# A low-rank weight mix: the plain weight enters the PSUM bank by a ScalarE copy in place of a VectorE addition

## The chip, the core and the metric

The kernel runs on one core of a Trainium2 chip. A core has five engines with queues of their own: TensorE (PE; its weight loads are listed as PEld), VectorE (DVE), ScalarE (ACT), GpSimd (POOL) and SyncE (SP), which here only issues transfers. TensorE writes its products into PSUM, a small memory of banks; a bank holds 128 partitions x 512 fp32 numbers. All other data on the core is in SBUF. The metric is the device time of one execution in microseconds (us), lower is better.

## The reference

```
x  : (2, 1024, 1024);  xn = layernorm(x)
s  = xn @ (weight * block_mask).T + bias                    # 32x32 blocks, about 0.3 of them on
coeffs[b] = softmax((mean_s(xn[b]) @ Wq.T) @ keys.T / sqrt(128))   # 8 experts
y  = xn @ W_org.T + sum_e coeffs[b, e] * (xn @ down[e]) @ up[e]    # rank 64 each
out = x + s * silu(y)
```

The sum over the experts is linear, so for each of the two batches (b = 0, 1) the kernel mixes one weight of 1024 x 1024, `W_org.T + down * (coeffs[b] * up)`, with `down` 1024 x 512 and `up` 512 x 1024, and then multiplies the activations by it. All of it is in fp32: the kernel splits each operand into a high part (rounded to the fp32r form that TensorE takes) and a low part (the rest), and makes three products per pair: high by high, high by low, low by high.

## The kernel before

**The mix.** A mixed weight is made in 16 pieces of 128 x 512: two halves of the columns (h = 0, 1), eight rows of tiles each (kt = 0 to 7). One piece goes through these functions:

- `y_prep` (line 373): SP loads the piece's `down` tile (`ds`) and the plain weight's piece (`wo`) into tiles of the pool `stage`, which has six tiles of one size, shared by all that is staged. ScalarE casts the high part (`dhi`, line 380), VectorE subtracts for the low part (`dlo`, line 381); each has two buffers.
- `y_mul` (line 384): 12 matmuls of 128 x 128 by 128 x 512 into one PSUM bank `psw` (two buffers): four groups of 128 ranks (the tiles `cut`, made by `scale_up`, lines 364 to 368, from the rows of `up` times the coefficients), three products each.
- `y_sum` (line 394): VectorE adds the bank to the plain weight's piece in SBUF (line 396).
- `y_hi` (line 398) and `y_lo` (line 405): for batch 0 the sum is split again, by a ScalarE cast (line 399) and a VectorE subtraction (line 407), into the weight slot that the later tiles multiply by. `y_add` is `y_sum` and `y_hi`, `y_fin` all three.

**The stages.** From the start to about 68 us the kernel loads, normalises and turns the activations and makes the masked product s of batch 0's first half of the columns. Then come:

1. The first mix (b, h) = (0, 0), lines 812 to 820: eight `y_mul` in a row, with each one's `y_sum`, the `y_prep` of the piece two on, `y_hi` and `y_lo` behind it.
2. The second mix (0, 1), `mix_jobs` and `jobs_b`: eight output tiles of 128 x 512 (24 matmuls each, `gemm`) that multiply by the first mixed weight, and after each of them one `y_mul`. A tile's evacuation and a piece's addition are put in a list `pending`, which `flush` issues ahead of the next tile.
3. Eight tiles that multiply by the second mixed weight, while VectorE, ScalarE and DMA prepare batch 1 (`wide_a`, `wide_b`: 1024-wide rows are normalised, added, and stored to a DRAM tensor `xv`) and the coefficients of batch 1.
4. The folds, `fold` (line 955): the 16 pieces of batch 1's mixed weight, in groups of 4, 4, 3, 3 and 2 with a tile of s (`s_tile`) ahead of each group. The sum is not split: it is stored from the `wo` tile to a DRAM tensor `yu` by a transfer that ScalarE issues one fold later (`store_late`). Between them stand `fill`s, which load prepared rows back and split them (lines 984 to 986). After the eighth fold `scale_up` makes the tiles `cut` for the other half of the columns, through four tiles of `stage`.
5. Batch 1's tiles (`quad`), from about 312 us to the end, which use a scheme with seven products in place of eight.

**What sets the order.** The whole body stands in a manual schedule: TensorE, VectorE, ScalarE and GpSimd run their instructions in the order in which the program issues them. Only SP's transfers, and which tile of a pool is handed out next, are placed by the framework. An engine that waits holds up all that stands behind it in its queue.

Of the kernel before, what the change touches and what calls it, by code (L numbers as in the profile page):

```python
# [9 lines left out]
F32 = mybir.dt.float32  # L10
# [4 lines left out]
ALU = mybir.AluOpType  # L15
AX = mybir.AxisListType

P = 128
# [4 lines left out]
NH = 512  # L23
# [9 lines left out]
def kernel(  # L33
# [26 lines left out]
    nc = tc.nc  # L60
# [23 lines left out]
    stage = for_fold("stage", 2)  # L84
    ps_acc = ctx.enter_context(tc.tile_pool(name="ps_acc", bufs=4, space=bass.MemoryType.PSUM))
    ps_w = ctx.enter_context(tc.tile_pool(name="ps_w", bufs=2, space=bass.MemoryType.PSUM))
# [101 lines left out]
    staged = {}  # L188
# [170 lines left out]
    def scale_up(b, h):  # L359
        cu[(b, h)] = []  # L360
        for c in range(4):
            t = cupool.tile([P, 2, NH], F32R, name="cut", tag="cu")
            st = stage.tile([P, NH], F32, name="us", tag="st", bufs=6)
            nc.sync.dma_start(st, up[c * P : (c + 1) * P, h * NH : (h + 1) * NH])
            s = csel[b][:, c : c + 1]
            hi = t[:, 0, :]
            nc.scalar.activation(hi, st, AF.Copy, scale=s)
            nc.vector.scalar_tensor_tensor(  # L368
                t[:, 1, :], st, s, hi.bitcast(F32), ALU.mult, ALU.subtract
            )  # L370
            cu[(b, h)].append(t)

    def y_prep(b, h, kt):
        ds = stage.tile([P, 4, P], F32, name="ds", tag="st", bufs=6)
        nc.sync.dma_start(ds, down[kt])
        ws = stage.tile([P, NH], F32, name="wo", tag="st", bufs=6)
        nc.sync.dma_start(ws, worgT[kt * P : (kt + 1) * P, h * NH : (h + 1) * NH])
        dhi = stage.tile([P, 4, P], F32R, name="dhi", bufs=2)
        dlo = stage.tile([P, 4, P], F32R, name="dlo", bufs=2)
        nc.scalar.copy(dhi, ds)  # L380
        nc.vector.tensor_tensor(dlo, ds, dhi.bitcast(F32), ALU.subtract)  # L381
        staged[(b, h, kt)] = dhi, dlo, ws

    def y_mul(b, h, kt):
        dhi, dlo, ws = staged[(b, h, kt)]
        u = cu[(b, h)]
        ps = ps_w.tile([P, NH], F32, name="psw", tag="psw")
        for c in range(4):
            nc.tensor.matmul(ps, lhsT=dhi[:, c, :], rhs=u[c][:, 0, :], start=c == 0, stop=False)  # L389
            nc.tensor.matmul(ps, lhsT=dhi[:, c, :], rhs=u[c][:, 1, :], start=False, stop=False)  # L390
            nc.tensor.matmul(ps, lhsT=dlo[:, c, :], rhs=u[c][:, 0, :], start=False, stop=c == 3)  # L391
        staged[(b, h, kt)] = ps, ws

    def y_sum(b, h, kt):
        ps, ws = staged[(b, h, kt)]
        nc.vector.tensor_tensor(ws, ws, ps, ALU.add)  # L396

    def y_hi(dst, b, h, kt):
        nc.scalar.copy(dst[:, kt, 0, :], staged[(b, h, kt)][1])

    def y_add(dst, b, h, kt):
        y_sum(b, h, kt)
        y_hi(dst, b, h, kt)

    def y_lo(dst, b, h, kt):
        ps, ws = staged.pop((b, h, kt))
        nc.vector.tensor_tensor(dst[:, kt, 1, :], ws, dst[:, kt, 0, :].bitcast(F32), ALU.subtract)

    def y_fin(dst, b, h, kt):
        y_add(dst, b, h, kt)  # L410
        y_lo(dst, b, h, kt)
# [44 lines left out]
    def tile_evac(kind, b, h, i, ps):  # L456
        mine = stash_p.tile([P, NH], F32, name="stash", tag="stash")
        if kind == "s":
            s_evac(mine, ps, b, i, h * NH, NH)
        else:  # L460
            y_evac(mine, ps, b, i)
        stash[(b, h, i)] = mine
# [14 lines left out]
    def store_late():  # L477

        while late_stores:
            nc.scalar.dma_start(*late_stores.pop(0))  # L480
# [3 lines left out]
    def flush():  # L484
        while pending:
            pending.pop(0)()
# [116 lines left out]
    with tc.manual_schedule(engines={mybir.EngineType.PE, mybir.EngineType.DVE, mybir.EngineType.Activation, mybir.EngineType.Pool}):  # L603
# [208 lines left out]
        for k in range(NKT):  # L812
            y_mul(0, 0, k)
            if k == 0:
                tile_evac("s", 0, 0, 7, q7)
            y_sum(0, 0, k)
            if k + 2 < NKT:
                y_prep(0, 0, k + 2)
            y_hi(y00, 0, 0, k)
            y_lo(y00, 0, 0, k)  # L820
# [132 lines left out]
        folds = [(h, kt) for h in range(2) for kt in range(NKT)]  # L953

        def fold(n):
            h, kt = folds[n]
            if n + 1 < len(folds):
                y_prep(1, *folds[n + 1])
            store_late()
            y_mul(1, h, kt)  # L960
            flush()
            y_sum(1, h, kt)
            ps, ws = staged.pop((1, h, kt))
            late_stores.append((
                yu[:, :, 2 * h + kt // 4, kt % 4, :].rearrange("u p n -> p u n"),
                ws.rearrange("p (u n) -> p u n", n=P),
            ))
            if n == NKT - 1:
                scale_up(1, 1)
# [297 lines left out]
```

## Time and profile before

| | us |
|---|---|
| median of 3 runs (461.96 to 462.08) | 461.96 |
| the profiled execution | 463.29 |
| its span, first to last instruction | 461.2 |
| TensorE busy | 443.0 |
| VectorE busy | 313.0 |
| ScalarE busy | 169.3 |

The span is a little shorter than the execution that it is from, since the time before the first and after the last instruction is not in it. Matmul rows overlap: each lasts about 0.39 us, and the next starts 0.227 us after it. In a line of the profile, `L396 DVE ... wo<-wo,psw ... x32 | 22.0, 686 | 17.3 <-PE psw L391 17.2` means: the instructions of line 396 on VectorE, which write `wo` and read `wo` and `psw`, 32 of them, busy for 22.0 us in all, 686 ns each; the engine was idle for 17.3 us just before them, of which 17.2 us ended when TensorE's line 391 had written `psw`. In a timeline the columns are start, length, engine, line, operation; the bracket at the end gives the idle time ahead of the instruction and what ended it.

### The profile page before, as it was taken

Reading aid. Unit: us, or ns where it says so; the run is one execution under the profiler, and the core shown is the slowest. Engines: PE = TensorE matmul, PEld = TensorE weight load, DVE = VectorE, ACT = ScalarE, POOL = GpSimd, SP = SyncE. Lnnn points to the kernel's source line nnn. Section 1 sums busy time; section 2 is a strip of 40 time slices with the busy share of each in tenths; the row PEclk is TensorE's granted clock in tenths of the full one; section 3 lists DMA queues with packets and bytes.
Section 4 is the critical chain, followed back from the end, with each engine's and each line's share of the span. In section 5 each row is a group of like instructions: output and inputs, shape, how many; then the busy total and the mean of one; then the engine's idle time right before and its main releaser. Section 6 shows DMA issues by size and latency. Waiting matters only on the chain.

```text
span 461.2 us, 5714 instructions
## 1 busy us (share of the span) xinstructions
PE 443.0 (96%) x2047; PEld 362.6 (79%) x2047; DVE 313.0 (68%) x504; ACT 169.3 (37%) x277; POOL 37.9 (8%) x40
## 2 busy tenths in 40 slices
PE   7799999999999999996999899999999999999996
PEld 5689888888887888874887688877888888888884
DVE  6989877667775788846555776769496196467624
ACT  4676534363223222214224223158343432441510
POOL 3884210000100000001000000000000000000000
PEclk9999999999999999998999999999999999999999
DMA  8996317687952688797887985664264134207003
GB/s 286 391 343 212 114 42 231 179 274 258 294 207 92 199 316 287 257 299 235 256 248 250 279 278 159 222 192 156 85 171 141 54 120 155 91 28 223 23 1 114
DMA packets 48172, 89.52 MB, mean 194 GB/s; under 512 B 4752, under 2 KB 14992, under 8 KB 48144
## 3 DMA queue, kind: packets, MB, share of 16 engines
q1 hardware_dynamic: 34512, 73.42, 49.1%
q10 hardware_dynamic: 13632, 15.73, 10.1%
q8 instruction: 16, 0.26, 0.2%
q14 instruction: 12, 0.10, 0.1%
HBM read 69.21 MB, written 19.92 MB: 193 GB/s over the span
## 4 chain that ended last, share of the span: by engine, by line
PE 74%; DVE 11%; DMA 10%; ACT 3%; issue 2%; SPq 0%; DVEq 0%; ACTq 0%
PE acc_ps L1127 22%; PE py L1127 9%; PE acc_ps L425 8%; PE acc_ps L427 8%; PE acc_ps L426 8%; PE psw L391 6%; PE psw L389 6%; PE psw L390 6%; DMA ws<-in_wT_dram 3%; DMA xv<-bd 2%; DMA xs<-xv 2%; DVE slot L544 1%; DMA raw<-in_x_dram 1%; DMA yu<-wo 1%; DMA us<-in_up_dram 1%
## 5 line engine op out<-in xcount | busy, mean ns | idle before, releaser
L1127 PE MATMUL acc_ps<-xw,ow 128*128 128x512 f32 x480 | 113.8, 393 | 0.7 <-ACT acc_ps L1158 0.4
L426 PE MATMUL acc_ps<-slot,xgrp 128*128 128x512 f32 (+1 forms) x288 | 105.8, 367 | 2.7 <-DVE slot L544 2.7
L1127 PEld LDWEIGHTS acc_ps<-xw,ow 128*128 128x128 f32 x480 | 90.0, 188 | 21.7 <-ACT acc_ps L1158 0.8
L425 PE MATMUL acc_ps<-slot,xgrp 128*128 128x512 f32 (+1 forms) x288 | 106.6, 370 | 0.1
L427 PE MATMUL acc_ps<-slot,xgrp 128*128 128x512 f32 (+1 forms) x288 | 105.6, 367 | 0.7 <-DVE xgrp L556 0.7
L426 PEld LDWEIGHTS acc_ps<-slot,xgrp 128*128 128x128 f32 x288 | 54.3, 189 | 12.2 <-DVE slot L544 3.6
L427 PEld LDWEIGHTS acc_ps<-slot,xgrp 128*128 128x128 f32 x288 | 54.2, 188 | 10.2 <-DVE xgrp L556 1.1
L425 PEld LDWEIGHTS acc_ps<-slot,xgrp 128*128 128x128 f32 x288 | 54.3, 188 | 9.1 <-DVE stash L439 0.3
L389 PE MATMUL psw<-cut,dhi 128*128 128x512 f32 x128 | 50.9, 398 | 4.5 <-ACT dhi L380 4.3
L391 PE MATMUL psw<-cut,dlo 128*128 128x512 f32 x128 | 50.9, 398 | 1.6 <-DVE dlo L381 1.5
L390 PE MATMUL psw<-cut,dhi 128*128 128x512 f32 x128 | 50.6, 395 | 0.0
L1127 PE MATMUL py<-xw,ow 128*128 128x512 f32 x192 | 46.9, 392 | 0.0
L1127 PEld LDWEIGHTS py<-xw,ow 128*128 128x128 f32 x192 | 36.1, 188 | 8.1
L1031 DVE TENSOR_TENSOR ow<-raw,ow 128x1024 fp32r<-128x1024 f32 (+1 forms) x32 | 34.5, 1089 | 11.2 <-ACT ow L1030 11.2
L380 ACT CAST dhi<-ds 128x512 fp32r<-128x512 f32 x32 | 19.8, 618 | 43.1 <-PE psw L390 24.3
L396 DVE TENSOR_TENSOR wo<-wo,psw 128x512 f32<-128x512 f32 x32 | 22.0, 686 | 17.3 <-PE psw L391 17.2
L389 PEld LDWEIGHTS psw<-cut,dhi 128*128 128x128 f32 x128 | 24.3, 190 | 10.2 <-ACT dhi L380 4.7
L391 PEld LDWEIGHTS psw<-cut,dlo 128*128 128x128 f32 x128 | 24.4, 191 | 8.4 <-DVE dlo L381 3.2
L1030 ACT CAST ow<-raw 128x1024 fp32r<-128x1024 f32 (+1 forms) x32 | 29.3, 939 | 2.0 <-DVE xw L986 2.0
L390 PEld LDWEIGHTS psw<-cut,dhi 128*128 128x128 f32 x128 | 24.3, 190 | 5.7 <-DVE cut L368 0.5
L381 DVE TENSOR_TENSOR dlo<-ds,dhi 128x512 fp32r<-128x512 f32 x32 | 21.9, 686 | 8.0 <-ACT dhi L380 8.0
L1172 DVE TENSOR_TENSOR py<-py,s 128x512 f32<-128x512 f32 x8 | 5.6, 699 | 29.6 <-ACT s L1134 29.4
(151 smaller groups left out, 451.6 us busy)
## 6 DMA issues: line engine op xcount, KB each, us to landing
ds<-in_down_dram SPq DMA_DIRECT2D x32, 256.0 KB, 3.7
wo<-in_worgT_dram SPq DMA_DIRECT2D x32, 256.0 KB, 3.9
raw<-in_x_dram SPq DMA_DIRECT2D x11, 512.0 KB, 6.3
res<-in_x_dram SPq DMA_DIRECT2D x16, 256.0 KB, 3.7
us<-in_up_dram SPq DMA_DIRECT2D x16, 256.0 KB, 3.6
out_dram<-res ACTq DMA_DIRECT2D x16, 256.0 KB, 3.6
raw<-in_wu_dram SPq DMA_DIRECT2D x8, 512.0 KB, 5.0
yu<-wo ACTq DMA_DIRECT2D x16, 256.0 KB, 4.0
```

Of the source, the lines that this page charges most:

```text
L380: nc.scalar.copy(dhi, ds)
L381: nc.vector.tensor_tensor(dlo, ds, dhi.bitcast(F32), ALU.subtract)
L389: nc.tensor.matmul(ps, lhsT=dhi[:, c, :], rhs=u[c][:, 0, :], start=c == 0, stop=False)
L390: nc.tensor.matmul(ps, lhsT=dhi[:, c, :], rhs=u[c][:, 1, :], start=False, stop=False)
L391: nc.tensor.matmul(ps, lhsT=dlo[:, c, :], rhs=u[c][:, 0, :], start=False, stop=c == 3)
L396: nc.vector.tensor_tensor(ws, ws, ps, ALU.add)
L425: nc.tensor.matmul(ps, lhsT=xs[:, kt, 0, cols], rhs=w[:, kt, 0, wc], start=kt == 0, stop=False)
L426: nc.tensor.matmul(ps, lhsT=xs[:, kt, 0, cols], rhs=w[:, kt, 1, wc], start=False, stop=False)
L427: nc.tensor.matmul(ps, lhsT=xs[:, kt, 1, cols], rhs=w[:, kt, 0, wc], start=False, stop=kt == NKT - 1)
L1030: nc.scalar.copy(o[:, a:b, 0], raw[:, a:b])
L1031: nc.vector.tensor_tensor(o[:, a:b, 1], raw[:, a:b], o[:, a:b, 0].bitcast(F32), ALU.subtract)
L1127: nc.tensor.matmul(ps, lhsT=o[:, a, wl, j, :], rhs=xw[j][:, m, xl, :], start=start and j == 0 and k == 0, stop=j == 3 and k == 2, skip_gro ...
```

## The change

The bank gets the plain weight first, by a ScalarE copy from SBUF (`y_seed`), and the matmuls then add to it: none of them starts the bank anew. The addition on VectorE goes. `y_hi` and `y_lo` read the sum from the bank itself. The first two pieces of the first mix stay as they were. Where no seed has been issued, `y_mul` issues it just ahead of its matmuls. In the folds the seed of the next piece is issued after this piece's matmuls, and as the sum is now in the bank, a ScalarE copy brings it to a new tile of `stage`, from which it is stored.

```diff
+    def y_seed(b, h, kt):
+        dhi, dlo, ws = staged[(b, h, kt)]
+        ps = ps_w.tile([P, NH], F32, name="psw", tag="psw")
+        nc.scalar.copy(ps, ws)
+        staged[(b, h, kt)] = dhi, dlo, ws, ps
+
     def y_mul(b, h, kt):
-        dhi, dlo, ws = staged[(b, h, kt)]
+        dhi, dlo = staged[(b, h, kt)][:2]
         u = cu[(b, h)]
-        ps = ps_w.tile([P, NH], F32, name="psw", tag="psw")
+        if (b, h) == (0, 0) and kt < 2:
+            ps = ps_w.tile([P, NH], F32, name="psw", tag="psw")
+        elif len(staged[(b, h, kt)]) == 3:
+            y_seed(b, h, kt)
+        seeded = len(staged[(b, h, kt)]) == 4
+        if seeded:
+            ps = staged[(b, h, kt)][3]
         for c in range(4):
...
+            for k, (d, ul) in enumerate(((dhi, 0), (dhi, 1), (dlo, 0))):
+                nc.tensor.matmul(
+                    ps, lhsT=d[:, c, :], rhs=u[c][:, ul, :], start=not seeded and c == 0 and k == 0, stop=c == 3 and k == 2,
+                    skip_group_check=seeded,
+                )
+        if not seeded:
+            ws = staged[(b, h, kt)][2]
+            nc.vector.tensor_tensor(ws, ws, ps, ALU.add)
+            ps = ws
+        staged[(b, h, kt)] = ps
 
-    def y_sum(b, h, kt):
-        ps, ws = staged[(b, h, kt)]
-        nc.vector.tensor_tensor(ws, ws, ps, ALU.add)
 
     def y_hi(dst, b, h, kt):
-        nc.scalar.copy(dst[:, kt, 0, :], staged[(b, h, kt)][1])
+        nc.scalar.copy(dst[:, kt, 0, :], staged[(b, h, kt)])
+
+    y_add = y_hi
 
     def y_lo(dst, b, h, kt):
-        ps, ws = staged.pop((b, h, kt))
-        nc.vector.tensor_tensor(dst[:, kt, 1, :], ws, dst[:, kt, 0, :].bitcast(F32), ALU.subtract)
+        ps = staged.pop((b, h, kt))
+        nc.vector.tensor_tensor(dst[:, kt, 1, :], ps, dst[:, kt, 0, :].bitcast(F32), ALU.subtract)
...
             y_mul(0, 0, k)
             if k == 0:
                 tile_evac("s", 0, 0, 7, q7)
-            y_sum(0, 0, k)
             if k + 2 < NKT:
                 y_prep(0, 0, k + 2)
             y_hi(y00, 0, 0, k)
...
             y_mul(1, h, kt)
+            if n + 1 < len(folds):
+                y_seed(1, *folds[n + 1])
             flush()
-            y_sum(1, h, kt)
-            ps, ws = staged.pop((1, h, kt))
+            ps = staged.pop((1, h, kt))
+            ws = stage.tile([P, NH], F32, name="wo", tag="st", bufs=6)
+            nc.scalar.copy(ws, ps)
             late_stores.append((
```

## The prediction

> **What bounds the kernel now.** I read the page's busy shares first, then the waits by releaser, then the busy time stage by stage, and last the timelines of the two stages that the edit touches. The page:
>
> ```profile
> PE 443.0 (96%) x2047; PEld 362.6 (79%) x2047; DVE 313.0 (68%) x504; ACT 169.3 (37%) x277; POOL 37.9 (8%) x40
> ...
> L389 PE MATMUL psw<-cut,dhi 128*128 128x512 f32 x128 | 50.9, 398 | 4.5 <-ACT dhi L380 4.3
> L391 PE MATMUL psw<-cut,dlo 128*128 128x512 f32 x128 | 50.9, 398 | 1.6 <-DVE dlo L381 1.5
> ...
> L380 ACT CAST dhi<-ds 128x512 fp32r<-128x512 f32 x32 | 19.8, 618 | 43.1 <-PE psw L390 24.3
> L396 DVE TENSOR_TENSOR wo<-wo,psw 128x512 f32<-128x512 f32 x32 | 22.0, 686 | 17.3 <-PE psw L391 17.2
> ```
>
> TensorE is the bound: every us in which it waits is a us of the kernel, and nearly nothing else counts. From 68 us on it waits in two places worth a sum: 4.3 us once (L389) and some 2 us around one fold (L391 above all). The additions to be removed (L396) wait for TensorE; TensorE waits for none of them beyond 0.2 us. So the edit has little to win, and the question is whether it makes TensorE wait. By stage (columns: stretch, length, busy us and instructions of PE, PEld, DVE, ACT, POOL, granted clock, DMA share, GB/s):
>
> ```profile
> 68.00:91.00 23.00, 23.00 (x102) 18.98 (x102) 17.12 (x26) 8.78 (x15) 0.00 (x0) 1.00 0.66 200
> 91.00:160.00 69.00, 68.67 (x323) 56.20 (x322) 47.72 (x88) 23.70 (x41) 4.41 (x8) 1.00 0.67 220
> 160.00:213.00 53.00, 49.30 (x222) 40.32 (x220) 38.47 (x64) 12.45 (x21) 1.65 (x1) 1.00 0.82 282
> 213.00:301.00 88.00, 85.35 (x362) 68.59 (x363) 56.45 (x83) 25.26 (x41) 0.00 (x0) 0.98 0.77 239
> ```
>
> They are: the first mix (8 products back to back, nothing else on TensorE), the second mix (one product after each tile), the tiles without a product, and the 16 folds. ScalarE is idle 62% of the first, so by shares it has room. Its order decides. One product's end there, in the timeline:
>
> ```profile
> 73.54 0.39 PE L391 MATMUL psw<-cut,dlo 128*128 128x512 f32 x1
> ...
> 73.77 0.39 PE L389 MATMUL psw<-cut,dhi 128*128 128x512 f32 x1
> 73.78 0.62 ACT L380 CAST dhi<-ds 128x512 fp32r<-128x512 f32 x1 [1.10 <-PE psw L390]
> ...
> 73.97 0.69 DVE L396 TENSOR_TENSOR wo<-wo,psw 128x512 f32<-128x512 f32 x1 [0.47 <-PE psw L391]
> ...
> 74.69 0.62 ACT L399 CAST slot<-wo 128x512 fp32r<-128x512 f32 x1 [0.28 <-DVE wo L396]
> ```
>
> Product 1's last matmul starts at 73.54; product 2's first follows at 73.77. Call such a moment E. The reader of the bank starts at E+0.20; the cast of the product after next (dhi) at E+0.01. Everything behind the product runs beside the next one.
>
> **The change, part by part.** Durations are of the profiled execution: 463.29 us, span 461.2, 1.33 above the median 461.96. Added waits are the same in either, so the sum goes on the median too.
>
> *Counts.* 30 of 32 additions leave VectorE (30 x 0.686 = 20.6 us). ScalarE gains 30 seeds (SBUF to bank) and 16 copies of a bank to a new staging tile. The trace has no copy from SBUF to a bank; nearest are bank to bank (L1158) 0.571 and SBUF to SBUF (L380) 0.618: I take 0.60, between two close ends. Back to back, ScalarE starts one every 0.53 (71.54, 72.07). After L1158's copy ended at 306.68 its matmul started at 306.73: 0.05. VectorE's freed time is worth nothing by itself, as TensorE did not wait for it. Casts and subtractions that now read the bank keep their prices (casts from a bank, L552, 0.583).
>
> *First mix.* In the built program ScalarE's order is: dhi(k+2), cast of product k, seed(k+1). So the seed of the next product stands behind a cast that waits for this product's end, and TensorE behind the seed. From E: dhi(k+2) at 0.01, cast at 0.54, seed at 1.07, done 1.67, matmul 1.72. Products 3 to 6: 4 x 1.72 = 6.9. Product 7 has no dhi in front (cast at 0.20): 1.38. Product 2 is the first seeded, and product 1 still goes through VectorE: addition 0.20, cast at 0.92 (74.69), seed at 1.45, matmul 2.10. Sum 10.3; with seeds of 0.571 and 0.618 and 0.1 of hand-over, 9.7 to 10.7. Nothing covers it: TensorE has no other work here.
>
> *Second mix.* Seed(i) stands behind dhi(i+1), but beside a tile of 24 x 0.227 = 5.44. After a product's end ScalarE has cast, evacuation, dhi and seed: 0.20 + 3 x 0.53 + 0.60 = 2.4, under 5.44: hidden. Not so for i=0: dhi(1) waits for its load. That load takes the slot of the first up row, free after VectorE's L368; it was asked for at 93.07 and cast at 96.81, 3.74 later. Product 7 ended at E=90.09. In the new order the cast comes 0.72 sooner, L368 ends at E+2.2, dhi(1) starts E+5.97, seed 0.53 later, matmul at E+7.15, due E+5.44: 1.7. From 0.5 (the load in 2.85, as at 212.30, is 0.8 off; seed 0.2 faster) to 2.4.
>
> *Third stage.* The chain of waits runs on VectorE, ScalarE and DMA from the addition at 158.97 (0.70) to the dhi at 213.24. That addition goes: the 4.3 us wait shrinks by 0.7; at least by nothing, as transfers fill most of the chain.
>
> *First fold.* The product started after dhi(0):
>
> ```profile
> 212.30 0.33 SPq L375 DMA_DIRECT2D ds<-in_down_dram  x1
> ...
> 213.24 0.60 ACT L380 CAST dhi<-ds 128x512 fp32r<-128x512 f32 x1
> 213.74 0.68 ACT L448 ACTIVATE stash<-acc_ps,rstd 128x512 f32<-128x512 f32 x1
> 215.15 0.62 ACT L380 CAST dhi<-ds 128x512 fp32r<-128x512 f32 x1 [0.72 <-DMA ds<-in_down_dram]
> ```
>
> Now seed(0) follows the second dhi: 215.68, matmul at 216.33 in place of 213.89, 2.44 later. All operands are there by then, which saves some 0.3 of the waits inside that product: 2.1 (1.0 if the load lands 1 us sooner, to 2.7).
>
> *Other folds.* Seed(n+1) is ahead of copy(n), so order costs nothing. But after E ScalarE has copy(n-1), in half the folds a fill's cast, dhi(n+1), the store's issue (0.4) and seed(n+1): 0.20 + 0.53 (+0.53) + 0.53 + 0.40 + 0.65 = 2.3 or 2.8 against 12 x 0.227 = 2.72. Products 2, 3, 6, 7 lose 0.1 to 0.25: 0.7. Queued behind such a late seed is copy(n), for which the store waits. And a fold now takes three of the six staging tiles, where it took two: SP asks for loads later. After the second up rows (fold 7), the operand of fold 9 gets the tile that fold 6's output leaves, whose store (4.0 us) is issued behind a dhi that itself waits for a load. Folds 8 to 10 now take 248.54 to 259.64, 11.1 for 36 x 0.227 = 8.16: 2.9 lost, by the late up rows and L1016. By hand I get 1.0, 1.7 and 1.85 lost at the three: 4.5, so 1.6 more. Both together 2.3, from 0 (every load in time) to +7.5 (each of three groups stalls like this one).
>
> Sum: 10.3 + 1.7 - 0.7 + 2.1 + 2.3 = **+15.7**: 479.0 for the profiled execution, **477.7** on the median. Low ends together +10.5 (472.5), high ends +23.3 (485.3).
>
> *The clock.* At 10 to 15 and 15 to 20 us TensorE is busy 3.50 and 3.35 of 5 us with gaps of 0.85 to 2.7, at a granted clock of 1.00. After the 4.3 us wait it is 0.55 for 3.6 us, matmuls 0.43 apart in place of 0.227. Gaps of 1.7 after 2.7 busy are like the first. I charge nothing. The Trainium skill ("TensorE: Matmul & The Clock Gate", section "A second HAM failure mode: psum-queue depth-cycling") holds that frequent short idles while cycling PSUM banks make the gate oscillate between half and full clock. By it the sum would rise by the first rival's price.
>
> **The rivals.**
> 1. The clock drops between the first mix's products: 6 x 12 x 0.2 = 14.6 more, 492. For: 213.8 to 217.4. Against: 10 to 20 us, and the gap before 257.24, after which matmuls come every 0.23.
> 2. Only a part of it: loads come in time in the folds and ahead of the second mix, and the casts and seeds overlap more closely than 0.53. 8 of the first mix, nothing else: 470.
> 3. The other side: ScalarE has each seed done before the previous product ends, and the removed additions shorten the third stage by 0.7 and end the 2.9 lost in folds 8 to 10: 458.4. It decides if seed(k+1) starts 0.65 or more before E; for it speak ScalarE's 62% idle time, against it the cast that waits for E in front of it.
>
> **How the numbers follow.** Forecast 79%, clock 8%, part 8%, other side 5%. Range: the forecast's bounds, lowered to the middle of rival 2 for its weight: 470 to 486; above lies the clock, below most of rival 3. A measurement of this kernel tells about 0.2% from no change; all but rival 3 are over that: slower 0.95, same 0.01, faster 0.04.
>
> **What would show it.** Right: in the first mix TensorE waits six times for ScalarE's copy into the bank (psw from wo), near 2.1, 1.7 four times and 1.4; one such wait near 1.7 before the second mix's first product; some 6 us in place of 4.3 before the folds, at its end the seed; no new wait in the third stage or after 313 us. Wrong: no wait on the seeds, a granted clock under 0.9 in the first mix, or waits in the later products of the second mix.

## The result and the profile after

The changed kernel takes 481.73 us (median of 4 runs, 479.08 to 483.96) against 462.02 of the kernel before on the same chip: a ratio of 1.0387, 95% interval 1.0340 to 1.0435. It is slower by 19.7 us; 477.7 was forecast, with 470 to 486 as the range. Measured again later it took 480.69 against 463.40: 1.0387 (1.0352 to 1.0422). The profiled execution took 479.08 us, span 477.0, so it is 2.65 us under the median of its own runs; that of before had a span of 461.2. The two spans differ by 15.8 us, where the sum forecast 15.7; that they agree so closely is in part luck, as the table below shows. Why the medians differ by more, 19.7 us, is taken up behind the experiments and stays open.

The page of the changed kernel, with the busy shares and the groups that answer to those shown of before (busy us, mean ns of one | idle time ahead, and what ended it):

```profile
PE 446.1 (94%) x2047; PEld 363.6 (76%) x2047; DVE 294.2 (62%) x474; ACT 191.2 (40%) x323; POOL 39.0 (8%) x40
...
L403 PE MATMUL psw<-cut,dhi 128*128 128x512 f32 x256 | 82.7, 403 | 18.4 <-ACT psw L388 18.1
...
L380 ACT CAST dhi<-ds 128x512 fp32r<-128x512 f32 x32 | 19.8, 619 | 33.1 <-DMA ds<-in_down_dram 20.3
...
L388 ACT COPY psw<-wo 128x512 f32<-128x512 f32 x30 | 17.7, 592 | 3.1 <-DVE dlo L381 1.4
```

VectorE's 18.8 us fewer and ScalarE's 21.9 us more say little: ScalarE is busy for 40% of the span. The second line says it all: the products' matmuls (L403) wait 18.4 us, 18.1 of them for the seed (L388). Before, L389 waited 4.5 us, 4.3 of them for the cast of a down row. A seed lasts 0.592 us; 0.60 was assumed.

By stage (columns as before: stretch, length, busy us and instructions of PE, PEld, DVE, ACT, POOL, granted clock, DMA share, GB/s; the stretches are the same work, later):

```profile
68.00:102.00 34.00, 24.95 (x104) 18.68 (x103) 14.13 (x22) 12.37 (x23) 0.00 (x0) 1.00 0.46 147
102.00:172.00 70.00, 68.93 (x323) 56.14 (x322) 42.43 (x80) 26.98 (x48) 5.53 (x8) 1.00 0.67 220
172.00:226.00 54.00, 50.15 (x227) 41.27 (x225) 39.96 (x66) 14.13 (x23) 1.65 (x1) 1.00 0.77 268
226.00:317.00 91.00, 86.25 (x364) 69.33 (x365) 45.65 (x65) 40.28 (x71) 0.00 (x0) 0.96 0.73 229
```

The first mix, where TensorE had not been idle, now has it idle for a quarter of the time, at a granted clock of 1.00. The end of product 2 in the timeline (start, us, instruction, idle time before and what ended it):

```profile
79.73 0.39 PE L403 MATMUL psw<-cut,dlo 128*128 128x512 f32 x1
79.97 0.62 ACT L380 CAST dhi<-ds 128x512 fp32r<-128x512 f32 x1 [2.93 <-PE psw L403]
80.49 0.58 ACT L414 CAST slot<-psw 128x512 fp32r<-128x512 f32 x1
...
80.97 0.59 ACT L388 COPY psw<-wo 128x512 f32<-128x512 f32 x1
...
81.62 0.73 PE L403 MATMUL psw<-cut,dhi 128*128 128x512 f32 x2 [1.50 <-ACT psw L388]
```

With E at 79.96, 0.23 after the last matmul's start, the cast of the product after next starts at E+0.01, the cast of the product's own sum at E+0.53, the seed at E+1.01 and TensorE at E+1.66. The prediction had 0.01, 0.54, 1.07 and 1.72. TensorE stands still while ScalarE does three copies in a row, of which it needs only the last, and that one could have been done before: its plain weight is there and its bank is free.

The wait that was 4.3 us before the folds, in the same view:

```profile
224.82 0.60 ACT L380 CAST dhi<-ds 128x512 fp32r<-128x512 f32 x1
225.33 0.68 ACT L461 ACTIVATE stash<-acc_ps,rstd 128x512 f32<-128x512 f32 x1
227.04 0.62 ACT L380 CAST dhi<-ds 128x512 fp32r<-128x512 f32 x1 [1.03 <-DMA ds<-in_down_dram]
227.56 1.10 ACT L388 COPY psw<-wo 128x512 f32<-128x512 f32 x2
...
228.20 1.22 PE L403 MATMUL psw<-cut,dhi 128*128 128x512 f32 x2 [6.05 <-ACT psw L388]
```

The first fold's down row was cast by 225.42. Its seed stands behind the next down row's cast, and that waits for a load.

So that runs can be compared by stage, this table cuts each profiled execution at TensorE's own marks: the first matmul of the first mix, the ends of the two mixes, the first matmul of the folds and the end of the 16th fold (us; the last column is the span less the rest).

| kernel | start | first mix | second mix | third stage | folds | after them |
|---|---|---|---|---|---|---|
| before | 68.28 | 21.81 | 68.68 | 55.12 | 70.34 | 177.0 |
| changed | 69.53 | 32.64 | 69.69 | 56.34 | 71.76 | 177.0 |
| changed, again (e0) | 68.17 | 32.69 | 70.55 | 55.98 | 73.30 | 177.8 |
| first mix's seeds ahead (e1) | 70.15 | 21.90 | 72.39 | 55.80 | 74.23 | 177.3 |
| first mix put back (e2) | 69.08 | 21.81 | 72.62 | 56.61 | 73.76 | 176.9 |
| all seeds ahead (e3) | 70.06 | 21.97 | 68.69 | 54.78 | 73.46 | 177.2 |
| seeds twice (e4) | 68.95 | 43.91 | 72.80 | 56.87 | 74.75 | 177.5 |
| folds put back, addition early (e5) | 69.87 | 32.71 | 71.14 | 55.87 | 73.87 | 176.7 |
| fold's sum in own tile (e6) | 71.72 | 32.67 | 72.70 | 57.06 | 69.64 | 177.6 |
| mixes ahead, folds as e5 (e7) | 70.43 | 21.96 | 68.69 | 53.10 | 75.06 | 177.0 |
| mixes ahead, folds of before (e8) | 70.35 | 22.05 | 68.69 | 53.34 | 71.34 | 176.6 |
| all ahead, own tile (e9) | 68.82 | 21.93 | 68.69 | 54.90 | 69.21 | 177.6 |
| first mix ahead, seeds twice (e10) | 69.80 | 24.18 | 71.10 | 55.45 | 72.95 | 177.0 |
| half a seed more (e11) | 68.78 | 40.78 | 70.35 | 58.29 | 72.59 | 176.7 |

Nothing that the change touches runs before the first mix, and the start still varies by 3.6 us. It makes 1.25 of the 15.8 us between the two profiles, and that is none of the change's doing: the stages that the change does touch became 14.5 us longer. The start goes with the clock: from 15 to 20 us it was 1.00 in before and 0.77 in the changed kernel, and the five profiles at a granted clock of 1.00 all the way (before, e0, e4, e9, e11) have starts of 68.17 to 68.95 us, the nine in which it drops somewhere between 5 and 25 us have 69.08 to 71.72.

### The profile page after: what moved, and what is told of

Read it like the earlier page. It is cut to its first block, busy times and chain, and to the rows that moved or that the text cites. A ratio compares the mean times of both kernels' runs of the same rounds, so it can differ in the third digit from the quotient of the medians.

```text
span 477.0 us, 5674 instructions
## 1 busy us (share of the span) xinstructions
PE 446.1 (94%) x2047; PEld 363.6 (76%) x2047; DVE 294.2 (62%) x474; ACT 191.2 (40%) x323; POOL 39.0 (8%) x40
## 3 DMA queue, kind: packets, MB, share of 16 engines
HBM read 69.21 MB, written 19.92 MB: 187 GB/s over the span
## 4 chain that ended last, share of the span: by engine, by line
PE 46%; issue 17%; DMA 9%; DVE 4%; ACT 3%; ACTq 0%; POOLq 0%; SPq 0%; POOL 0%; DVEq 0%
PE acc_ps L1142 21%; PE psw L403 9%; PE py L1142 9%; DMA ds<-in_down_dram 3%; PE acc_ps L439 3%; PE acc_ps L440 3%; PE acc_ps L438 3%; DMA xs<-xv 2%; DMA out_dram<-res 1%; DVE st L144 1%; DMA raw<-in_x_dram 1%; ACT psw L388 1%; DMA us<-in_up_dram 1%; DMA yu<-wo 1%; ACT dhi L380 1%
## 5 line engine op out<-in xcount | busy, mean ns | idle before, releaser
L403 PE MATMUL psw<-cut,dhi 128*128 128x512 f32 x256 | 82.7, 403 | 18.4 <-ACT psw L388 18.1
L403 PEld LDWEIGHTS psw<-cut,dhi 128*128 128x128 f32 x256 | 48.3, 192 | 33.8 <-ACT psw L388 22.8
L403 PE MATMUL psw<-cut,dlo 128*128 128x512 f32 x128 | 50.8, 397 | 0.0
L1046 DVE TENSOR_TENSOR ow<-raw,ow 128x1024 fp32r<-128x1024 f32 (+1 forms) x32 | 34.5, 1088 | 10.7 <-ACT ow L1045 10.6
L403 PEld LDWEIGHTS psw<-cut,dlo 128*128 128x128 f32 x128 | 24.5, 191 | 5.6 <-DVE dlo L381 0.2
L414 ACT CAST slot<-psw 128x512 fp32r<-128x512 f32 x14 | 8.2, 585 | 33.8 <-PE psw L403 33.8
L1039 DVE TENSOR_TENSOR raw<-raw 128x512 f32<-128x512 f32 x32 | 21.4, 687 | 0.5
L388 ACT COPY psw<-wo 128x512 f32<-128x512 f32 x30 | 17.7, 592 | 3.1 <-DVE dlo L381 1.4
```

The lines of the kernel that those rows point to most:

```text
L388: nc.scalar.copy(ps, ws)
L403: nc.tensor.matmul(ps, lhsT=d[:, c, :], rhs=u[c][:, ul, :], start=not seeded and c == 0 and k == 0, stop=c == 3 and k == 2, skip_group_che ...
L414: nc.scalar.copy(dst[:, kt, 0, :], staged[(b, h, kt)])
L1039: nc.vector.tensor_tensor(raw[:, o], raw[:, a], raw[:, b], op)
L1046: nc.vector.tensor_tensor(o[:, a:b, 1], raw[:, a:b], o[:, a:b, 0].bitcast(F32), ALU.subtract)
```

## The experiments

The theory: the seed itself is cheap, and its place in ScalarE's order costs: behind a cast that waits for a product or for a load. Its rivals: the copy costs wherever it stands; the clock is the larger part; the folds' loads are the larger part. Times of e0 to e3 compare with 480.69 of e0 and with 463.40 of before in the same series; in the later series before took 464.47 (e4 to e7) and 463.98 (e8 to e11).

**e0: the changed kernel again.**

> The changed kernel once more, unaltered. Its four runs lay at 479.08 to 483.96 us, and only the fastest was profiled, whose lost time is accounted for. Theory: the other 2 to 5 us lie in stretches where the granted clock is below 1.00 (the mean clock fell from 0.989 to 0.977 with the time), in the first 30 us or around the 6 us wait before the folds; the first mix takes 32.6 us again. Rival: they lie in the folds, where an operand's load that comes late holds a product up; then the five groups of folds take more than 13.1, 10.9, 11.5, 9.0 and 5.5 us at an unchanged clock.

480.69 us (480.07 to 482.46). The profiled execution, 480.56, began the first mix 1.4 us sooner than the first one and still ended later: 0.9 us went in the second mix, whose first product waited 1.60 us in place of 0.74, 1.5 in the folds, 0.8 behind them, all at a mean clock of 0.992, which was 0.987 in the first one. So in this execution it was not the clock. The rival is right in part: the second and third group of folds took 11.27 and 12.86 us, over its bounds, the other three (12.95, 8.94 and 5.49) stayed within them. Two things came later: in the second mix a load, for which TensorE waits by way of a seed, and in the folds above all the late up rows, for which product 8 waits without any seed (4.86 us in place of 3.65). The theory's clock is seen in the runs below.

**e1: the first mix's seeds ahead of the casts.**

```diff
             y_mul(0, 0, k)
             ...
+            if 2 <= k + 1 < NKT:
+                y_seed(0, 0, k + 1)
             if k + 2 < NKT:
                 y_prep(0, 0, k + 2)
             y_hi(y00, 0, 0, k)
```

> In the first mix the seed of the next product is issued ahead of the cast of the product after next and of the cast of the one that just ended; the same instructions, nothing else moved. Theory (the order costs, not the copy): the seed needs a bank that VectorE's subtraction left some 2.05 us after the product before ended, so it is done at 2.65 of the 2.72 us that a product takes; the 10.0 us that TensorE lost in the first mix fall to 0 to 2, the mix takes 21.8 to 24 us in place of 32.6, and the time falls by 8 to 10 us, to 472 to 474. Rival (the copy itself costs: ScalarE is too full, or its writes into the banks hold TensorE up): the mix still takes over 29 us, and the time stays over 478.

472.99 us (469.78 to 473.88), 7.7 less than e0. ScalarE's copies in the timeline of e1, with the same columns as above:

```profile
78.37 0.62 ACT L380 CAST dhi<-ds 128x512 fp32r<-128x512 f32 x1 [0.71 <-PE psw L403]
78.89 0.58 ACT L414 CAST slot<-psw 128x512 fp32r<-128x512 f32 x1
80.35 0.59 ACT L388 COPY psw<-wo 128x512 f32<-128x512 f32 x1 [0.88 <-DVE slot L420]
81.09 0.62 ACT L380 CAST dhi<-ds 128x512 fp32r<-128x512 f32 x1
```

The same seeds, on the same engine; each waits for VectorE's subtraction to leave its bank (L420) and is done at 80.94, as TensorE comes free. The first mix takes 21.90 us, 0.1 more than before the change. In this mix the order cost 10.7 us, and the copy next to nothing. But the time fell by 7.7, not by 10: the second mix became 1.8 us longer than in e0. Its first product, in the timeline of e1:

```profile
99.46 1.05 PE L403 MATMUL psw<-cut,dhi 128*128 128x512 f32 x2 [1.79 <-ACT psw L388]
100.31 0.63 PE L403 MATMUL psw<-cut,dlo 128*128 128x512 f32 x1
100.73 1.06 PE L403 MATMUL psw<-cut,dhi 128*128 128x512 f32 x2
```

It waits 1.79 us for its seed, and after that two matmuls take 0.85 us from start to start where they took 0.45: half clock. The product lasts 4.46 us in place of 2.76. The same happens after a wait of 1.95 us in the folds.

**e2: the first mix put back to VectorE's additions.**

```diff
-        if (b, h) == (0, 0) and kt < 2:
+        if (b, h) == (0, 0):
             ps = ps_w.tile([P, NH], F32, name="psw", tag="psw")
```

> All eight products of the first mix are added by VectorE as before the change; the second mix and the folds stay changed. Theory: the first mix is two thirds of the loss, so it takes 21.8 us again and the time falls by 10 to 11 us, to 471 to 472; the 0.9 us before the second mix, the 6.2 us before the folds and the folds stay as they are. Rival (the folds' loads or the clock are most of the loss in the median): the time falls by under 8 us.

473.27 us (472.85 to 475.27), 7.4 less than e0. The first mix takes 21.81 us again, to the hundredth. As in e1 some 3 us come back by half clock: after a wait of 2.09 us ahead of the second mix and of 1.81 in the folds. The theory's stage was right, its time 1.3 us too low, for that reason; the rival's bound (under 8 us less) was met, though the first mix is still the largest part of the loss, and it named the right place, the folds and the clock, for the remainder.

**e3: every seed that TensorE would wait for is put ahead.** On top of e1:

```diff
             if i == 0:
                 y_prep(b, h, 0)
+                y_seed(b, h, 0)
             if i + 1 < NKT:
                 y_prep(b, h, i + 1)
...
         y_prep(1, *folds[0])
+        y_seed(1, *folds[0])
```

> The seeds of the first mix ahead of both casts, and also the first seed of the second mix and the first seed of the folds ahead of the cast for the product that follows. Theory: on top of the 8 to 10 us of the first mix this takes back the 0.9 us before the second mix and 1.8 of the 6.2 us before the folds, so 10.5 to 12.5 us less than the changed kernel, 469 to 471; the rest, 1 to 2 us, stays in the folds. Rival (what ends those two waits is the late load, not the seed): as with the first mix's seeds alone, within 1 us.

467.95 us (464.81 to 471.08), 12.7 less than e0, a little more than expected, and 1.0097 (1.0058 to 1.0137) of before. The second mix takes 68.69 us, as before the change, so both its loss and its half clock were the seed's place. The wait before the folds fell from 6.05 to 4.50 us. By median 4.6 us against before are left. Of the 5.0 us between the profiled executions 1.8 are the start and 3.1 the folds, all of that in products 8 to 10: 14.42 us in place of 11.10, with half clock after a wait of 2.08 us.

**e4: the seeds of batch 0 twice.**

```diff
         nc.scalar.copy(ps, ws)
+        if b == 0:
+            nc.scalar.copy(ps, ws)
```

> The changed kernel with every seed of batch 0 (6 in the first mix, 8 in the second) issued twice into the same bank; the second copy writes the same values, so nothing else changes. Theory (the seed is on the path in the first mix and at the head of the second, and hidden elsewhere): each of the six losses of the first mix grows by one ScalarE interval, 0.53: 10.0 becomes 13.2 and the mix 35.8 us; the second mix loses 0.5 more at its first product and nothing at the other seven; 3.7 us in all. Rival (writes into a bank hold TensorE up, wherever they stand): the seven later products of the second mix slow down too, by 0.1 to 0.5 each, and the second mix takes over 72 us at a clock of 1.00.

496.98 us (one run): 16.3 more than e0 where 3.7 was expected. The waits did what the theory says: 2.07 us in place of 1.50. The seven later products of the second mix with their tiles take 60.76 us in place of 60.47, so writes into the banks hold TensorE up by 0.04 us each at most; e10, with the same copies, has 60.47. What came on top is half clock, in the stretch that holds products 2 to 6 (columns as in the stages above):

```profile
74.00:110.00 36.00, 23.50 (x63) 16.38 (x61) 8.31 (x13) 12.71 (x23) 0.00 (x0) 0.76 0.32 95
```

and, in products 2 and 3, in the timeline of e4:

```profile
77.13 0.80 PE L405 MATMUL psw<-cut,dhi 128*128 128x512 f32 x2 [2.54 <-ACT psw L390]
77.73 0.63 PE L405 MATMUL psw<-cut,dlo 128*128 128x512 f32 x1
78.16 1.06 PE L405 MATMUL psw<-cut,dhi 128*128 128x512 f32 x2
...
80.72 0.79 PE L405 MATMUL psw<-cut,dhi 128*128 128x512 f32 x2
81.34 0.39 PE L405 MATMUL psw<-cut,dlo 128*128 128x512 f32 x1
83.81 0.73 PE L405 MATMUL psw<-cut,dhi 128*128 128x512 f32 x2 [2.08 <-ACT psw L390]
```

From about 77.7 to 81 the matmuls are 0.43 apart, then 0.23 until the next wait, and from about 84.5 they are 0.43 apart again. The first mix takes 43.91 us: 32.69, six times 0.57 for the longer waits, and some 7.8 of half clock. This is the prediction's first rival, which the changed kernel misses by half a microsecond of idle time per product. e10 and e11 ask whether it is the idle time.

**e10: the first mix's seeds ahead, and twice.** The edits of e1 and e4 together.

> Seeds of the first mix ahead of the casts, and every seed of batch 0 issued twice into the same bank. Theory (the half clock of the run with doubled seeds came from the idle time of 2.1 to 2.5 us ahead of each product, not from the copies): the second copy ends about 0.5 us after TensorE is due, so the mix takes 22 to 26 us, with a granted clock of 1.00. Rival (twice the writes into the banks slow TensorE down): matmuls 0.3 to 0.43 us apart in the mix as there, over 30 us.

472.64 us in all (one run). The first mix takes 24.18 us. Its waits are 0.07 to 0.34 us, and its stretch runs at full clock with as many copies as in e4:

```profile
69.80:94.00 24.20, 23.39 (x98) 17.64 (x97) 12.67 (x20) 14.62 (x27) 0.00 (x0) 1.00 0.69 206
```

So it is not the copies that bring half clock, but TensorE's idle time.

**e11: half a seed more behind each product.**

```diff
         nc.scalar.copy(ps, ws)
+        if (b, h) == (0, 0):
+            nc.scalar.copy(ps[:, : NH // 2], ws[:, : NH // 2])
```

> The changed kernel, with half of each seed of the first mix (256 of 512 columns) issued a second time: about 0.35 us more behind each product, so TensorE idles 1.8 to 1.9 us in place of 1.5 (2.3 before product 2, 1.5 before product 7). Theory (the clock halves for 3.4 us after an idle time of 2.07 us or more, and between 1.8 and 2.0 only in some cases): half clock after product 2's gap, and after some of the four others: the mix takes 36 to 44 us. Rival (the doubled run's half clock has nothing to do with the length of the gap but with a second copy of the whole bank): a granted clock of 1.00 throughout, and 34.7 us.

The first mix takes 40.78 us (489.56 us in all, one run). Half clock followed the waits of 2.33, 1.77, 1.87 and 1.86 us, and not those of 1.67 and 1.63. A third of a microsecond of copy per product costs 8.1 us, about 2 of them as waits.

The waits of TensorE of 1 us and more between 56 and 330 us, over all 14 profiles, come out like this:

| idle time | full clock after it | half clock, within the next 3.3 us |
|---|---|---|
| 1.08 to 1.67 us | 30 | 1 |
| 1.77 to 2.54 us | 11 | 18 |
| 2.82 to 7.19 us | 0 | 14 |

Length alone does not decide the middle row: 2.17 us was followed by full clock in e5, 1.77 by half clock in e11. That half clock always follows 2.07 us or more, as e11's text supposed, is refuted by the 2.17 of e5 and by 2.14 in e10. The cases are not independent either: 20 of the 30 in the first row and four of the 11 in the second are the first mix in the four profiles in which it is the changed kernel's.

The traces show more than the lengths. In all of them the granted clock changes only at the edges of windows of 3.41 us, which lie elsewhere from run to run: every stretch at half clock lasts 3.41 us or a multiple of it, but for the last one, which the end of the trace cuts off. Four of these windows of e4, then two of the changed kernel's first mix (columns as in the stages):

```profile
74.24:77.65 3.41, 0.87 (x4) 0.48 (x3) 2.20 (x4) 2.31 (x4) 0.00 (x0) 1.00 0.73 196
77.65:81.06 3.41, 3.41 (x9) 2.68 (x9) 0.00 (x0) 0.00 (x0) 0.00 (x0) 0.50 0.65 189
81.06:84.48 3.42, 1.34 (x6) 0.77 (x5) 1.29 (x2) 2.18 (x4) 0.00 (x0) 1.00 0.13 40
84.48:87.89 3.41, 3.41 (x10) 2.66 (x9) 0.00 (x0) 0.00 (x0) 0.00 (x0) 0.50 0.35 117
...
75.70:79.11 3.41, 2.01 (x9) 1.67 (x10) 1.50 (x3) 1.11 (x2) 0.00 (x0) 1.00 0.83 260
79.11:82.52 3.41, 1.91 (x9) 1.27 (x8) 1.29 (x2) 1.59 (x3) 0.00 (x0) 1.00 0.37 122
```

Take all windows at full clock from 56 to 330 us in the 14 profiles. Where TensorE was busy for under 0.40 of one, the next was at half clock in 23 of 23 cases; from 0.40 to 0.51 in 10 of 13; above that in none of 1028. So a wait near 2 us counts in full when it lies within one window, and is shared out when it lies across an edge: the 2.17 us of e5 leave TensorE busy for 1.84 us of the one window and 2.81 of the next. This was read from the traces behind the runs; no run was made to test it.

**e5: the folds put back.**

```diff
-        if (b, h) == (0, 0) and kt < 2:
+        if b == 1 or ((b, h) == (0, 0) and kt < 2):
             ps = ps_w.tile([P, NH], F32, name="psw", tag="psw")
...
             y_mul(1, h, kt)
-            if n + 1 < len(folds):
-                y_seed(1, *folds[n + 1])
             flush()
-            ps = staged.pop((1, h, kt))
-            ws = stage.tile([P, NH], F32, name="wo", tag="st", bufs=6)
-            nc.scalar.copy(ws, ps)
+            ws = staged.pop((1, h, kt))
```

> The 16 folds as before the change (VectorE's addition, the sum in the plain weight's tile); both mixes stay changed. Theory: the wait before the folds falls from 6.1 to about 4.4 us and the folds take 70 to 71 us again in place of 72 to 74 (first product to the end of the last), so the time falls by 3 to 5 us, to 475 to 477.5. Rival (the wait is the operands' load and the folds' loss is the late up rows, both there before): 478 to 480, with the wait still over 5.5 us.

481.59 us (477.64 to 482.60): a miss. The wait before the folds did fall, to 4.63 us, and is ended by the cast of the down row again; but the folds took 73.87 us. The edit was not what its text said: the addition sits in `y_mul`, and so stands on VectorE ahead of the work that `flush()` issues; before the change it stood behind. e8 corrects that.

**e6: a fold's sum in the tile of its plain weight.**

```diff
-        staged[(b, h, kt)] = ps
+        staged[(b, h, kt)] = ps if b == 0 else (ps, staged[(b, h, kt)][2])
...
-            ps = staged.pop((1, h, kt))
-            ws = stage.tile([P, NH], F32, name="wo", tag="st", bufs=6)
+            ps, ws = staged.pop((1, h, kt))
             nc.scalar.copy(ws, ps)
```

> The changed kernel, but a fold's sum is copied from the bank into the tile that its plain weight came in, so that a fold takes two of the six staging tiles, as before the change, in place of three. Theory of the prediction (the third tile makes loads late): folds 8 to 10 lose 2.9 us as before in place of 3.3 to 6.3, and the time falls by 0.5 to 3 us. Rival (fold 10's load waits for the tile of fold 7's sum, whose store is issued behind the casts of the up rows whichever tile it is): folds 8 to 10 lose over 3.3 us still, TensorE waits some 1.8 to 2.1 us there for a seed, and the time stays within 1 us of the changed kernel.

480.05 us (476.53 to 483.53): by its time, within 1 us of e0, no verdict. By its stages there is one: the folds take 69.64 us, and products 8 to 10 take 9.73, where the changed kernel took 11.49 and 12.86; both of the rival's signs in the folds are missing. The gain does not show in that execution since it started 3.6 us later than e0 and had half clock after a wait of 2.09 us in the second mix.

**e7: seeds ahead in both mixes, VectorE's additions in the folds** (e3's edits for the mixes and e5's for the folds).

> Seeds in both mixes of batch 0, each ahead of the casts and of the first late load; the 16 folds by VectorE as before. Theory: the mixes cost nothing, the third stage keeps its 0.3 to 0.7 us, and with the folds of before the time is that of the kernel before, or up to 0.7 us less: 462 to 463.5. Rival (something of the seeds stays on the path in the mixes): 465 or more.

467.97 us (465.81 to 468.95), 1.0069 (1.0036 to 1.0102) of before: a miss of the theory, and not for the rival's reason. The mixes cost nothing, the third stage even became 2.0 us shorter, and the folds took 75.06 us, with the same early addition as in e5.

**e8: as e7, with the addition where it was before the change.**

```diff
+        if b == 1:
+            staged[(b, h, kt)] = ps, staged[(b, h, kt)][2]
+            return
         if not seeded:
...
             flush()
-            ws = staged.pop((1, h, kt))
+            ps, ws = staged.pop((1, h, kt))
+            nc.vector.tensor_tensor(ws, ws, ps, ALU.add)
```

> Seeds ahead in both mixes, and the folds now exactly as before the change: VectorE's addition stands behind the work that had been put off until after the product (in the two runs with the folds put back it had slipped ahead of it). Theory (the slip is what made those folds 73.9 and 75.1 us long): folds 70 to 71.5 us, mixes 22.0 and 68.7, third stage 53 to 55; the time is that of the kernel before, or up to 2 us less. Rival (the folds' length has nothing to do with the place of the addition, but with what the freed VectorE lets happen sooner): folds 73 to 75 us again and the time 3 to 5 us over the kernel before.

465.09 us (12 runs), 1.0012 (0.9977 to 1.0046) of before: no difference. The folds took 71.34 us. The second and fourth of their five groups (of 4, 4, 3, 3 and 2) are at 10.92 and 8.20 us, as in before; with the early addition they were at 11.5 and 9.4 in both runs. So an addition that waits for TensorE, ahead of VectorE work that doesn't, cost the folds 1.8 us in these two groups. It does not explain all of e7's 75.06: there the third group ran into half clock as well.

**e9: all seeds ahead, and the sum in its own tile** (the edits of e3 and e6).

> Every seed of a first or back-to-back product ahead of the casts, and a fold's sum copied into its plain weight's tile: both of the losses that the runs so far show in the changed kernel are taken away, the seeds stay. Theory: mixes 22.0 and 68.7 us, third stage 54.8, folds 68.7 to 69.7 (with products 8 to 10 at 9.7), so 0.5 to 1.8 us less than the kernel before. Rival (the short folds 8 to 10 of the earlier run were a lucky landing of loads): folds 72 to 74.5 us, 3 to 5 us over the kernel before.

464.53 us (12 runs) against 463.98 of before (23 runs): 1.0002 (0.9977 to 1.0028), that is from 1.1 us less to 1.3 more. The table has its folds at 69.21, with products 8 to 10 at 10.19, and its mixes and third stage within 0.3 us of before. SyncE's queue around products 8 to 10 in the timeline of e9, where product 8 starts at 248.77 (ds are the down rows of products 9, 10 and 11, wo plain weights, misc the fills that `fill` loads for later products):

```profile
246.40 0.33 SPq L375 DMA_DIRECT2D ds<-in_down_dram  x1
248.63 0.33 SPq L377 DMA_DIRECT2D wo<-in_worgT_dram  x1
249.29 0.33 SPq L375 DMA_DIRECT2D ds<-in_down_dram  x1
250.93 0.33 SPq L377 DMA_DIRECT2D wo<-in_worgT_dram  x1
253.80 0.33 SPq L375 DMA_DIRECT2D ds<-in_down_dram  x1
254.18 0.42 SPq L1001 DMA_DIRECT2D misc<-xv  x1
```

and in the timeline of the changed kernel, where product 8 starts at 263.12:

```profile
261.96 0.33 SPq L375 DMA_DIRECT2D ds<-in_down_dram  x1
262.48 0.33 SPq L377 DMA_DIRECT2D wo<-in_worgT_dram  x1
266.77 0.33 SPq L999 DMA_DIRECT2D misc<-xv  x1
267.15 0.42 SPq L375 DMA_DIRECT2D ds<-in_down_dram  x1
...
270.03 0.33 SPq L999 DMA_DIRECT2D misc<-xv  x1
270.40 0.43 SPq L375 DMA_DIRECT2D ds<-in_down_dram  x1
```

Set against the start of product 8, the three down rows are asked for at -2.4, +0.5 and +5.0 us in e9 (in before, at -2.3, +0.7 and +5.1), and at -1.2, +4.0 and +7.3 in the changed kernel. The load of product 10 goes out 0.38 us after a fill's, and that fill waited for its buffer, as VectorE's and ScalarE's part of the timeline of the changed kernel shows:

```profile
264.64 0.72 ACT L367 ACTIVATE cut<-us,c 128x512 fp32r<-128x512 f32 x1 [0.59 <-DMA us<-in_up_dram]
265.27 0.60 ACT L1000 CAST xw<-misc 128x512 fp32r<-128x512 f32 x1
...
266.06 0.68 DVE L1001 TENSOR_TENSOR xw<-misc,xw 128x512 fp32r<-128x512 f32 x1
...
271.74 0.73 PE L403 MATMUL psw<-cut,dhi 128*128 128x512 f32 x2 [1.79 <-ACT psw L388]
```

The earlier fill's last reader (L1001) ends at 266.74, behind the late up rows; 0.03 us later the next fill's load is issued, then product 10's. The staging tile itself was free: in the built program it is one that the third up row had left, whose last reader ended at 264.83. So it is SyncE's order. That order is not written out but placed by the framework, and with the third tile per fold it puts the fill's load ahead of product 10's, where with two tiles (before, e6, e9) it stands behind two more down rows. The shorter folds are shown twice, by e6 and e9; that this order and nothing else makes them so is read from the trace, and was not tried alone.

That e9 would be faster than the kernel before is not shown: e8 and e9, without and with seeds in the folds, both end at no difference. No version here beats the kernel before.

## Why the prediction was right, and where it was not

Between the two profiles the first mix, the second mix, the third stage with the first fold, and the other folds lost 10.8, 1.0, 1.5 and 1.2 us, where 10.3, 1.7, 1.4 and 2.3 were forecast: together 14.5 and 15.7. The two largest gaps are in the second mix and the other folds. The median is 4 us above the forecast, and no run shows where those lie.

**What bounds the kernel** was right: TensorE's waits account for the result, and VectorE's 18.8 freed us were worth nothing. With every seed out of the way and two staging tiles per fold (e9), the change is a change of nothing.

**First mix, +10.3 (9.7 to 10.7): right.** The six losses are 2.08, 1.66, 1.61, 1.66, 1.66 and 1.33 us, 10.0 together; predicted were 2.10, four of 1.72, and 1.38. ScalarE's step from a cast out of the bank to the seed is 0.48, not 0.53. The mix itself became 10.8 us longer: after each wait a product takes some 0.13 more, as its first two matmuls last 0.73 and not 0.62. That term was missing. e1 and e2 show the cause.

**Second mix, +1.7 (0.5 to 2.4): the mechanism was right, the size varies.** The loss ahead of the first product was 0.9 us in the profiled run, 1.8 in e0, and in e5 and e6, which have the same code up to there, 2.3. The later products lost nothing, as said; e3 takes all of it away. Missing was what the clock adds: in e1, e2 and e6 another 1.7.

**Third stage and first fold, -0.7 and +2.1: right.** The third stage with the wait became 1.2 us longer and the first group of folds 0.3, together 1.5 (in e0 1.0) where 1.4 was forecast. e3 and e9, with the folds' first seed ahead, tell the two terms apart: there the two stretches together take 0.6 and 0.4 us less than before the change, and the changed kernel takes 2.1 and 1.9 more than they do. Without seeds in the folds the wait before them is 2.82 and 3.06 us in e7 and e8, whose mixes have their seeds ahead, but 4.63 in e5, whose mixes do not; which of the loads came sooner was not looked into.

**Other folds, +2.3 (0 to 7.5): inside a wide range, and in part wrong in how.** They lost 1.2 us in the profiled run and 2.9 in e0. Of that, products 8 to 10 have 0.4 and 1.8, where 1.6 was forecast, and products 11 to 13, of which nothing was said, 0.76 and 0.74. The 0.1 to 0.25 us forecast for products 2, 3, 6 and 7 are 0 in the one and at most 0.35 in the other. For products 8, 9 and 10 the prediction had losses of 1.0, 1.7 and 1.85 us; in the profiled run they are 0.9, 0.3 and 2.1. Product 9's load did wait for the tile that product 6's sum leaves, as forecast. It goes out at 261.96, when the store of that sum has landed; SyncE's waits from 261.5 to 262.4 (who waited for what: us in total, times, longest):

```profile
SPq L375 <- DMA yu<-wo: 0.6, 1, 0.6
```

It cost little. The large loss is product 10's, and there the detail was wrong: its load waits for no such tile but stands in SyncE's queue behind a fill's, with its own tile free since 264.83. Among products 11 to 13 TensorE waits 0.47 us for the seed of product 13, which stands behind the issue of two stores; in e1 to e4 and e11, with the same folds, these are issued earlier, the seed comes 1.4 us sooner, and the group takes 8.20 us as before. For products 8 to 10 the third tile is the cause all the same, by the order of SyncE's queue: with it taken away (e6, e9) they take 9.73 and 10.19 us, with it 11.49 to 14.42 in eight profiles (some of them with half clock), and the folds are 0.7 and 1.1 us shorter than before the change.

**The clock, charged nothing: it held in both profiles of the changed kernel, but the reason given was wrong.** The row of 10 to 20 us was misread: TensorE's idle times there are 0.57 to 1.07 us, not 0.85 to 2.7, and so say nothing of gaps of 1.7; the same stretch later showed 0.77 at the same busy time. By the windows of 3.41 us the waits of 1.2 to 1.5 us in the first mix are short enough: they leave TensorE busy for 0.56 of a window or more. Waits of 1.77 to 2.54 us were followed by half clock in 18 of 29 cases, for 3.41 us, which costs up to 1.7 us each. The changed kernel has three waits that can reach that length. Product 2's, of 1.92 us, was followed by full clock in all four profiles that have it. The second mix's first product ran into half clock in e6, and a product among 8 to 10 in e1 and e2, with the same code there; that neither happened in the two profiles of the changed kernel is chance. Whether this is what lifts the unprofiled runs to 484 is not shown, as no such run has a trace: two of the three have a lower mean clock (0.985 and 0.977) than the profiled one's 0.987, the third a higher one (0.989) and is slower too.

The rule weighed in the prediction, of the Trainium skill's page "TensorE: Matmul & The Clock Gate", section "A second HAM failure mode: psum-queue depth-cycling", would have brought half clock into the first mix. The changed kernel does not show that (idle 1.17 to 1.92 us per product, clock 1.00), e4 and e11 do (1.63 to 2.54, clock 0.76 and 0.79 over the products): the pattern alone does not decide, how long TensorE idles matters too. The same page, section "HAM oscillation — how this bites in real kernels", gives as its rule of thumb that TensorE should not idle longer than about 3.4 us. Here 1.8 us was at times enough.

**The rivals.** The first, the clock, had the right place for a kernel whose waits are 0.3 to 0.6 us longer (e11, e4), but its 14.6 us were too much: half clock cost about 6 and 7.8 us there, since it lasts for a part of each product only. The second, only part of the sum, is refuted by the stages. The third, seeds done before the product ends, is what e1 and e3 build by hand: its condition for the first mix holds there (in e1 the seed starts at 80.35, 0.72 us before the next product), and the mix comes back to its length before, not below it.

## What to carry to other kernels

When an operation moves from behind a product to ahead of it, look at what stands in front of it on its new engine: a copy that nothing delays costs nothing, and the same copy behind a cast that waits for the last product costs its own time, that of the cast and all that is between. Issue a seed as soon as its bank is free, ahead of work that waits for TensorE or for a load. And where TensorE is the bound, price a wait of some 2 us at what follows it too: half clock for the next 3.4 us may nearly double it, in one run and not in another.

## What the runs showed of the hardware that was not expected

- Half clock follows idle times of TensorE in 18 of 29 cases between 1.77 and 2.54 us, in all 14 of 2.82 us and more, and in 1 of 31 below 1.7 (e7, after 1.42 us). In the changed kernel, TensorE idle for 1.5 us in every 4.5 stays at full clock; with 1.86 in a row of such waits (e11) it does not. The clock changes at the edges of windows of 3.41 us, and what goes before half clock is a window in which TensorE is busy for less than about half of the time (33 of the 36 at 0.51 or less, none of the 1028 above).
- The first matmuls after a wait are slower at full clock as well: two in 0.73 us in place of 0.62. The extra time is in the first of them, 0.50 us in place of 0.39 (the same in before, after the wait that ends at 257.24).
- The same start of 68 us, untouched by any edit, took 68.17 to 71.72 us: the granted clock at 15 to 20 us was 1.00 in before and e0, 0.68 in e2, and 0.77 in the changed kernel's first profile, whose row of that stretch (columns as in the stages) is

```profile
15.00:20.00 5.00, 3.37 (x18) 3.01 (x17) 4.95 (x7) 1.47 (x3) 3.49 (x3) 0.77 1.06 370
```

  with TensorE as busy as in before, 3.35 of 5 us.

- A copy by ScalarE into a bank beside TensorE's matmuls into the other bank cost TensorE nothing that can be seen: seven products of the second mix with their tiles take 60.47 us with two copies for each (e10), as with one (e0).
